# Two lanes of images: stating the first three blocks of a lane's next image ahead of the other lane's bilinear block

## The chip, the cores and the metric

The kernel runs on one core of a Trainium2 chip. The metric is device time in microseconds (us) of one execution. Three runs of the kernel before gave 13435.75, 13443.8 and 13488.92 us; their median, 13443.8 us, is the time before.

## What is computed

Sixteen images of 56 x 56 pixels and 128 channels, all float32, pass one after the other through four residual layers. Each layer normalizes its input by groups of four channels, applies a block and adds the result back:

```python
x = x + _L0(_gn(x), ...)   # attention in shifted 7x7 windows, 4 heads
x = x + _L1(_gn(x), ...)   # triangle multiplication: gated projections, one 56x56 product per channel, layer norms
x = x + _L2(_gn(x), ...)   # Fourier attention over channels and two spectral operators with GELU
x = x + _L3(_gn(x), ...)   # bilinear: per-pixel 16x8 and 16x16 products of convolved keys and values
return x
```

The images do not touch each other anywhere, so the order in which they are worked on is free. Within an image every layer needs the whole result of the layer before.

## The kernel before, in words

An image stays in on-chip memory as a tile `xt` (128 channels x 3136 pixels) from its load to its store. There are two **lanes**; image b belongs to lane b mod 2 (`lane[0] = b % 2`, line 466). Each lane has buffers of its own: one large scratch tile, the arena (lines 321 and 335), five 512-column work tiles (`w2`), twelve scratch buffers in device memory (`dram`), two small PSUM buffers (`psb`) and one double-size PSUM buffer (`psd`). The pool of image tiles has two buffers that the lanes share (line 320). Since a lane has one arena and every block takes it anew, the blocks of one lane follow each other. Only work of the other lane can stand beside them, so there are at most two images in flight.

The four blocks, with the names used below:

- **Window attention** (`_window_attention`, lines 480 to 612): eight rows of windows. TensorE makes queries, keys, values and scores (line 563 is the score product), VectorE does the softmax, ScalarE copies.
- **Triangle** (`_triangle`, lines 615 to 726): many small TensorE products (line 678 makes the gated projections) and VectorE gates (lines 689 and 690).
- **Fourier** (`_fourier`, lines 729 to 1273): after attention over channels (line 1093), an inner loop of 64 steps. Each step fetches two pieces of a coefficient table by GpSimd DMAs (line 1200), multiplies them on VectorE (line 1202) and sums on TensorE (line 371, the helper `together`). It ends with two spectral operators and adds its parts to `xt` at lines 1253 and 1271.
- **Bilinear** (`_bilinear`, lines 1276 to 1472): seven chunks of 448 pixels. `project` (line 1317) makes queries, keys and values and writes copies to device memory by DMAs on ScalarE's queue. `spread` (line 1372) reads shifted planes back on SyncE's queue. `contract` (line 1399) reads a query or kernel tile back four times on SyncE's queue (line 1408), multiplies on VectorE (line 1411, 84 instructions for each image) and sums on TensorE. `last` (line 1426) stores the chunk (line 1445), so this block also writes the output.

What sets the order: the program only states instructions. When it is built, a scheduler walks them with an estimate of each duration and places each on its engine's list when its operands and buffers would be there. Among instructions that could go next on an engine, the one stated earlier goes first. The lists are fixed from then on, and each engine takes its own list in order. The statement order of the images is therefore a priority. In the kernel before, all four blocks of image b are stated ahead of everything of image b+1 (lines 465 to 472):

```python
    for b in range(NB):
        lane[0] = b % 2
        xt = load_image(b)
        done = False
        for s in stages:
            done = run[s](b, xt)
```

Of the kernel before, what the change touches and what calls it, by code (L numbers as in the profile page):

```python
# [307 lines left out]
def tile_blocks(ctx: ExitStack, tc: tile.TileContext, ins, out, at, stages=(0, 1, 2, 3)):  # L308
    nc = tc.nc
    x_in = ins["x"]  # L310
    NB = x_in.shape[0]
# [16 lines left out]
    lane = [0]  # L328
    count = [0]

    def uid(s):
        count[0] += 1
        return f"{s}{count[0]}"
# [4 lines left out]
    def w2():  # L338
        return w2p[lane[0]].tile([P, 512], F32, tag="w2", name=uid("w2_"))
# [4 lines left out]
    def psb():  # L344
        return ps1[lane[0]].tile([P, 512], F32, tag="ps1", name=uid("psb"))
# [37 lines left out]
    def W(name):  # L383
        rows, o, n = at["wgt"][name]
        return wgt[:rows, o : o + n]
# [47 lines left out]
    def load_image(b):  # L433

        xt = xpool.tile([P, NTOK], F32, tag="xt", name=uid("xt"))
        for q in range(NCH):
            t = w2()
            tv = t[:TT, :].rearrange("p (a c) -> p a c", a=4)
            nc.sync.dma_start(
                out=tv,  # L440
                in_=xf[b, q * CH : (q + 1) * CH, :].rearrange("(a p) c -> p a c", p=TT),
            )
            p = psb()
            for a in range(4):
                nc.tensor.transpose(p[:, a * TT : (a + 1) * TT], tv[:, a, :], ident[:TT, :TT])
            act(xt[:, q * CH : (q + 1) * CH], p[:, :CH], AF.Identity, bias=W("bout0"))
        return xt

    def store_image(b, xt):
        for q in range(NCH):  # L450
            p = psb()
            for a in range(4):
                o = q * CH + a * TT
                nc.tensor.transpose(p[:TT, a * P : (a + 1) * P], xt[:, o : o + TT], ident)
            t = w2()
            nc.scalar.copy(t[:TT, :], p[:TT, :])
            nc.sync.dma_start(
                out=of[b, q * CH : (q + 1) * CH, :].rearrange("(a p) c -> p a c", p=TT),
                in_=t[:TT, :].rearrange("p (a c) -> p a c", a=4),
            )  # L460
# [1 line left out]
    env = dict(locals())  # L462
    blocks = [_window_attention, _triangle, _fourier, _bilinear]
    run = {s: blocks[s](env) for s in stages}
    for b in range(NB):
        lane[0] = b % 2
        xt = load_image(b)
        done = False
        for s in stages:
            done = run[s](b, xt)  # L470
        if not done:
            store_image(b, xt)


class _Env:
# [1008 lines left out]
def _build(inputs, bacc, stages=(0, 1, 2, 3)):  # L1484
    x = np.ascontiguousarray(inputs["x"])
    w, early, late = _weights({k: v for k, v in inputs.items() if k != "x"})
    arrays, at = {"x": x}, {}
    for name, parts in (("cst", _constants()), ("wgt", w), ("early", early), ("late", late)):
        arrays[name], at[name] = _pack(parts)
    nc = bacc.Bacc("TRN2", target_bir_lowering=False, num_devices=1)  # L1490
    ins = {k: nc.dram_tensor(k, v.shape, F32, kind="ExternalInput").ap() for k, v in arrays.items()}
    out = nc.dram_tensor("out", x.shape, F32, kind="ExternalOutput").ap()
    with tile.TileContext(nc, schedule_with_timeline_sim=True) as tc:
        tile_blocks(tc, ins, out, at, stages)
    return nc, arrays, out, at
```

## Time and profile before

| What | Value |
|---|---|
| median of three runs | 13443.8 us |
| the profiled execution | 13405.75 us, span 13403.8 us |
| TensorE matmul busy | 10585.8 us, 79% of the span |
| VectorE busy | 9623.6 us, 72% |
| ScalarE busy | 3845.7 us, 29% |
| GpSimd busy | 1426.4 us, 11% |
| moved by DMA | 2105.94 MB, 157 GB/s on the mean |
| granted TensorE clock, mean | 0.847 of full speed |

The page divides the span into 40 slices and gives each engine's busy share in tenths. The pattern repeats about every five slices, once for each pair of images, eight pairs in all. The trace also answers for any stretch of time: busy time of each engine, the granted clock, and the share of the DMA engines in use. Where the stretch is limited to one line of the program, it counts that line's instructions, and so shows which block is at work and how far it gets. Two marks place the images in time: the DMAs of line 439 (seven for each image, its load) and those of line 1445 (seven for each image, its store).

### The profile page before, as it was taken

The page shows a single profiled execution, that of the slowest core. Times are in us where ns is not written, and L with a number is a line of the kernel's source. Part 1 is how long each engine was busy: PE and PEld are TensorE (multiplying, and loading weights), DVE is VectorE, ACT ScalarE, POOL GpSimd, SP SyncE. Part 2 cuts the span into 40 slices and gives each one's busy share as a digit, 9 for nine tenths or more (in the row PEclk, how much of TensorE's full clock was granted, in tenths as well). Part 3 has the DMA queues.
Part 4 walks back from the last instruction along what each step waited for, and adds up shares of the span by engine and source line. Part 5 has one row for each costly group of instructions (what it writes and reads, how often), then busy time and mean ns, then how long its engine had stood idle before and what let it go on. Part 6 is the DMA issues. An engine that isn't in the chain of part 4 may idle for free. (4 is left out here: it accounts for less than half of the span.)

```text
span 13403.8 us, 202422 instructions
## 1 busy us (share of the span) xinstructions
PE 10585.8 (79%) x82624; PEld 5860.7 (44%) x82624; DVE 9623.6 (72%) x13985; ACT 3845.7 (29%) x6638; POOL 1426.4 (11%) x2746
## 2 busy tenths in 40 slices
PE   7887687876878778887778877888778887788776
PEld 4454254542544335443355433554335443354432
DVE  7776868667677686676766667767777677866776
ACT  3223141321423224232242222422224232242221
POOL 0120002200022000220002200022000220002200
PEclk9988898878988889888888778888888888888887
DMA  1256904468044680447804468044780447704577
GB/s 35 73 164 230 315 1 118 118 244 300 1 124 124 237 294 9 118 138 240 276 10 118 131 228 291 13 118 130 245 279 10 118 136 252 270 7 118 131 249 267
DMA packets 1091758, 2105.94 MB, mean 157 GB/s; under 512 B 98320, under 2 KB 974096, under 8 KB 1089680
## 3 DMA queue, kind: packets, MB, share of 16 engines
q1 hardware_dynamic: 560000, 823.95, 18.7%
q0 software_dynamic: 165120, 629.61, 17.1%
q10 hardware_dynamic: 365712, 639.44, 13.2%
q8 instruction: 654, 10.72, 0.3%
q14 instruction: 272, 2.23, 0.1%
HBM read 1412.73 MB, written 667.03 MB: 155 GB/s over the span
## 5 line engine op out<-in xcount | busy, mean ns | idle before, releaser
L1411 DVE TENSOR_TENSOR arena<-arena 128x1792 f32<-128x1792 f32 x1344 | 2661.8, 2018 | 724.6 <-DMA arena<-dy 329.5
L1202 DVE TENSOR_TENSOR arena<-arena 112x1344 f32<-112x1344 f32 x1024 | 1569.5, 1552 | 356.8 <-DMA arena<-table 341.1
L371 PE MATMUL psb<-arena,cst 128*32 128x448 f32 x9792 | 1578.0, 672 | 0.0
L368 PE MATMUL psb<-arena,cst 128*32 128x448 f32 x1408 | 818.8, 670 | 799.9 <-DVE arena L1411 750.3
L1200 POOL DMA_DIRECT2D arena<-table x2048 | 1063.7, 521 | 2799.3 <-PE psb L1116 724.8
L371 PE MATMUL psb<-arena 112*64 112x224 f32 (+2 forms) x4864 | 1245.2, 525 | 0.0
L368 PE MATMUL psb<-arena 112*64 112x448 f32 (+1 forms) x1280 | 691.4, 625 | 369.2 <-DVE arena L1093 187.5
L371 PE MATMUL psd<-arena 112*64 112x224 f32 (+1 forms) x3072 | 749.4, 465 | 0.0
L368 PE MATMUL psd<-arena 112*64 112x448 f32 x1024 | 554.5, 627 | 211.4 <-DVE arena L1202 190.9
L1093 DVE TENSOR_TENSOR arena<-w,coef 128x1792 f32<-128x1792 f32 x256 | 507.6, 2020 | 210.7 <-PE psb L371 187.4
L371 PEld LDWEIGHTS psb<-arena 112*64 112x64 f32 (+1 forms) x4864 | 435.6, 153 | 509.7 <-issue 507.3
L368 PEld LDWEIGHTS psb<-arena,cst 128*32 128x32 f32 x1408 | 118.4, 119 | 1154.3 <-DVE arena L1411 869.2
L678 PE MATMUL psd<-wgt,arena 128*64 128x128 f32 x7168 | 514.4, 293 | 112.4 <-DVE arena L690 96.5
L371 PEld LDWEIGHTS psb<-arena,cst 128*32 128x32 f32 x9792 | 367.6, 125 | 471.4 <-issue 451.0
L1396 ACT COPY arena<-psd 128x896 f32<-128x896 f32 x336 | 303.4, 905 | 930.8 <-DVE arena L1411 549.4
L678 PEld LDWEIGHTS psd<-wgt,arena 128*64 128x64 f32 x7168 | 450.0, 145 | 217.1 <-issue 129.2
L907 PE MATMUL psb<-cst,arena 128*128 128x64 f32 (+1 forms) x2688 | 454.9, 341 | 92.4 <-ACT arena L917 63.2
L371 PE MATMUL psd<-arena,wgt 128*32 128x448 f32 x2688 | 500.6, 604 | 34.4 <-DMA arena<-padded 34.0
L907 PEld LDWEIGHTS psb<-cst,arena 128*128 128x128 f32 x2688 | 437.2, 254 | 148.8 <-ACT arena L917 74.0
L1313 ACT COPY w<-psb 128x448 f32<-128x448 f32 x336 | 178.6, 532 | 1089.1 <-PE psb L371 761.8
L368 PE MATMUL psd<-arena,wgt 128*32 128x448 f32 x896 | 438.6, 607 | 42.4 <-DMA arena<-padded 37.4
L371 PEld LDWEIGHTS psd<-arena 112*64 112x64 f32 x3072 | 287.0, 151 | 284.4 <-issue 283.0
(299 smaller groups left out, 19594.2 us busy)
## 6 DMA issues: line engine op xcount, KB each, us to landing
arena<-table POOLq DMA_DIRECT2D x2048, 294.0 KB, 8.7
dy<-w ACTq DMA_DIRECT2D x336, 1792.0 KB
arena<-dy SPq DMA_DIRECT2D x1344, 448.0 KB
arena<-padded SPq DMA_DIRECT2D x896, 162.8 KB
w<-x SPq DMA_DIRECT2D x112, 224.0 KB
out<-w SPq DMA_DIRECT2D x112, 224.0 KB
padded<-w ACTq DMA_DIRECT2D x336, 62.0 KB
arena<-arena POOLq DMA_DIRECT2D x16, 784.0 KB, 9.8
```

Source lines behind the costliest of these rows:

```text
L368: done = mm(**first)
L371: mm(**kw)
L678: mm(p[half : half + 64, i // 4, i % 4 * P : (i % 4 + 1) * P], lhsT=xh[:, c0 : c0 + 64], rhs=W(w).rearrange("p (k c) -> p k c", c=64)[:, : ...
L907: mm(p[:, 2 * i * nl : 2 * (i + 1) * nl], lhsT=src[:, t * P : (t + 1) * P], rhs=fc, start=True, stop=True)
L1093: tt(t4, bc(ys[c][:, l0 : l0 + 4, :], 1, 8), bc(coef[:, c, h0 : h0 + 8, l0 : l0 + 4], 3, T), ALU.mult,)
L1200: nc.gpsimd.dma_start(out=t[hh * T : (hh + 1) * T, :], in_=bc(tflat[q, two, hh], 0, T))
L1202: tt(t4, bc(x3[:, :, s], 1, 2), t4, ALU.mult)
L1313: nc.scalar.copy(t[:, :CH], p[:, :CH])
L1396: nc.scalar.copy(z, p[:, :, :CH])
L1411: tt(t4, bc(rep, 2, 2), bc(z, 1, 2), ALU.mult)
```

## The change

The loop over images is split in two functions. `first(b)` loads image b and states its first three blocks; `second(b)` states its bilinear block. The loop states `second(b - 2)` and then `first(b)`:

```diff
-    for b in range(NB):
+    early = [s for s in stages if s < 3]
+    late = [s for s in stages if s >= 3]
+    images = {}
+
+    def first(b):
         lane[0] = b % 2
-        xt = load_image(b)
-        done = False
-        for s in stages:
+        images[b] = load_image(b)
+        for s in early:
+            run[s](b, images[b])
+
+    def second(b):
+        lane[0] = b % 2
+        xt, done = images.pop(b), False
+        for s in late:
             done = run[s](b, xt)
         if not done:
             store_image(b, xt)
+
+    for b in range(NB + 2):
+        if b >= 2:
+            second(b - 2)
+        if b < NB:
+            first(b)
```

With F for load and first three blocks and B for the bilinear block, the order of statement was F0 B0 F1 B1 F2 B2 F3 B3 and so on. It becomes F0 F1 B0 F2 B1 F3 B2 F4 and so on, ending with F15 B14 B15. Within a lane nothing changes its place: lane 0 is F0 B0 F2 B2 in both. No instruction is added or removed, and no buffer changes. What changes is which lane goes first where one lane has a B and the other an F to do: before, the lower image number; now, the F.

## The prediction

> **What bounds the kernel now.** I read the page's first two parts, then stretches of time by engine and by line, then the waits, then SyncE's timeline.
>
> ```profile
> span 13403.8 us, 202422 instructions
> ...
> PE 10585.8 (79%) x82624; PEld 5860.7 (44%) x82624; DVE 9623.6 (72%) x13985; ACT 3845.7 (29%) x6638; POOL 1426.4 (11%) x2746
> ...
> DVE  7776868667677686676766667767777677866776
> ...
> DMA  1256904468044680447804468044780447704577
> ```
>
> No engine is full over the span. The DMA row runs 0, 4, 4, 6 to 7, 8 in every five slices, again and again: the two lanes go through the same blocks at nearly the same time. That comes to one pair of images in about 1655 us: the first loads of lane 0 (line 439) stand at 18, 1587, 3243, 4824, 6431, 8165, 9822 and 11478 us, and lane 0 stores last at 13142. Lane 1 loads 7, 72, 94, 191, 263, 213, 222 and 217 us after lane 0. So lane 0's lead grows to about 220 us and stays there.
>
> Now six stretches, named by what the lanes do: both in bilinear (first pair), lane 0 in window attention beside lane 1's bilinear end, lane 0 in bilinear beside lane 1's Fourier end, both in bilinear (last pair), and image 15 alone in bilinear.
>
> ```profile
> core 0: us, PE busy (x) PEld busy (x) DVE busy (x) ACT busy (x) POOL busy (x), PEclk, DMA share, GB/s
> 1144.00:1530.00 386.00, 300.07 (x1853) 130.07 (x1848) 267.36 (x309) 73.57 (x125) 5.57 (x11) 0.85 0.95 336
> 11478.00:11695.00 217.00, 154.53 (x1230) 66.06 (x1222) 175.74 (x187) 49.21 (x86) 14.56 (x16) 0.89 0.81 267
> ...
> 12683.00:12966.00 283.00, 228.51 (x1535) 122.97 (x1535) 191.40 (x349) 91.04 (x158) 9.68 (x16) 0.82 0.61 208
> 12966.00:13142.00 176.00, 130.36 (x772) 53.05 (x772) 130.09 (x157) 30.10 (x53) 5.50 (x6) 0.82 0.89 309
> 13142.00:13400.00 258.00, 162.56 (x976) 58.10 (x976) 163.66 (x121) 31.76 (x49) 1.01 (x2) 0.77 0.75 255
> ```
>
> The same stretches for line 1411, VectorE's product of the bilinear block, 84 for each image:
>
> ```profile
> 1144.00:1530.00 386.00, 222.83 (x115) 0.85 0.95 336
> 11478.00:11695.00 217.00, 125.49 (x64) 0.89 0.81 267
> ...
> 12683.00:12966.00 283.00, 85.74 (x43) 0.82 0.61 208
> 12966.00:13142.00 176.00, 102.92 (x52) 0.82 0.89 309
> 13142.00:13400.00 258.00, 145.10 (x73) 0.77 0.75 255
> ```
>
> This is the heart of it. Two bilinear blocks together make 115 / 386 = 0.298 products per us, or 52 / 176 = 0.295. One alone makes 73 / 258 = 0.283. One beside window attention makes 64 / 217 = 0.295. A second bilinear block adds nothing: with two, the DMA engines are 0.89 to 0.95 busy and every product waits for its data. Beside window attention the same rate is had with the DMA at 0.81, and the other lane gets on too. How far is told by its score product (line 563, 128 records for each image):
>
> ```profile
> 11478.00:11695.00 217.00, 7.03 (x64) 3.89 (x64) 0.89 0.81 267
> ```
>
> 64 of 128: half a window attention, in time in which a second bilinear block would have given nothing. The waits name the same loop, and the timeline of SyncE shows what lane 0's next load stands behind:
>
> ```profile
> PE psb L368 <- DVE arena L1411: 750.3, 335, 11.2
> ...
> DVE arena L1411 <- DMA arena<-dy: 329.5, 157, 10.5
> ```
>
> ```profile
> 1529.77 0.34 SPq L1445 DMA_DIRECT2D out<-w  x1
> ...
> 1586.77 4.23 SPq L439 DMA_DIRECT2D w<-x  x4
> ```
>
> Image 0 is stored at 1529.77, but image 2's load goes out only at 1586.77, after image 1's bilinear transfers on the same list.
>
> **What the skill says.** "Perfetto Trace Analysis", section "Optimization Strategy": where a kernel has several regimes with different busiest engines, "performance may be improved by interleaving those regimes in addition to optimizing within each regime". The trace agrees that there are regimes: DMA 0.95 with both lanes in bilinear, 0.02 from 11708 to 11946 with both in the first two blocks. The same page, "Engine Utilization", gives 358 GB/s as the memory's full rate; the 336 GB/s above are 94% of it. "PSUM — Partial Sum Buffer", section "Engine vs sequencer instructions", says that "ScalarE/VectorE/GpSimdE queues are strict FIFO". That is why statement order matters here: a 2.0 us product (line 1411) placed ahead on VectorE holds up the small instructions of the other lane. "TensorE: Matmul & The Clock Gate", section "What's actually happening", has the clock halved when TensorE has been idle. The trace fits: 0.77 with bilinear alone, 0.92 from 11708 to 11946.
>
> **The change, part by part.** No instruction is added or taken away, so no duration of a row changes. The price is in order only.
>
> 1. F2 against B1 (and every like pair): the load, its seven DMAs on SyncE, the memsets on GpSimd (lines 520, 525, 658) and window attention now go ahead of the other lane's bilinear end. Before, window attention of lane 0 took 195 us in the first pair (VectorE's line 415, one at the head of each block, at 47 and 241) and 285 us in the last (11521 to 11806), where it stood behind bilinear. Lane 0 should get most of these 90 us back in each pair. What is queued behind it: bilinear's read-backs (line 1408) behind seven loads, 0.31 to 0.43 us of SyncE each, some 3 us; and products of line 1411 behind window attention's VectorE work. Image 13's bilinear end then takes perhaps 20 to 60 us longer.
> 2. The load's delay: 1586.77 - 1529.77 = 57 us in the first pair, 43 in the second (3200 to 3243), none later, where loads go out up to 29 us before the last store. It falls on one lane of two: (57 + 43) / 2 = 50 us saved.
> 3. B0 against F1: the Fourier end now goes ahead of bilinear's start. Before, with bilinear ahead, lane 1's Fourier took 702 us in the last pair (line 415 at 12275 and 12977) against 613 and 682 in the first. I count this at nothing; it is hidden as long as bilinear waits for DMAs. If that cover fails, bilinear's start loses up to the same 90 us, half of it for the pair. On GpSimd the table DMAs (line 1200) go ahead of bilinear's memset (line 1360): 0.5 us each, 128 for an image, but spread over the inner loop; counted at nothing as well.
> 4. The lead. In the first pair lane 0 gains about 80 us by the end of Fourier (line 415 at 1051 and 1144) and 136 by the last store (1530 and 1666). Part 1's priority took that back to 72. Now it stays, and part 1 adds to it: I estimate a lead of 130 us at the second pair, 250 at the third, and over 400 from the fourth on, past the length of a bilinear block (456 to 511 us).
> 5. What the lead is worth. As it grows, time with both in bilinear (176 us in the last pair, 231 to 264 in the three before, about 220) goes over into bilinear beside the first blocks. 217 us of that kind gave half a window attention free: half of its 200 us in lockstep, on one lane of two, so 50 us for 217, or 51 for 220. Bounds: nothing, if the added contention eats it, and 111, if the block that goes first runs at about twice that pace. I take 55, a little over the measured mean, since F goes first.
> 6. The end. Image 15's bilinear block stands alone there. It took 258 us after image 14; now the whole block is alone: about 93 us to its first products (line 415 at 1051, lane 1 in bilinear at 1144) and 84 / 0.283 = 297, so 390. Cost 390 - 258 = 132 us.
>
> Sum: the saving of 55 counts half in the second pair and whole in six, 6.5 x 55 = 358. 13406 - 358 - 50 + 132 = 13130 for the profiled execution. The median of the runs stands 38 us (0.28%) above it, so 13130 x 1.0028 = 13167; I say **13165 us**, 2.1% below.
>
> **Rivals.**
>
> *More:* F, going first, runs near the pace it would have alone, the upper bound of step 5. 13406 - 6.5 x 111 - 50 + 132 = 12766, times 1.0028 = 12800. For it: TensorE is 0.71 and VectorE 0.81 busy beside window attention, so there is room. Against: their sum, 1.52, is hardly more than the 1.47 of two bilinear blocks.
>
> *Nothing moves:* the builder's estimate may see little of the DMA's limit, and order decides only where two instructions are ready at once. In the kernel before, strict priority for the lower image gave lane 0 just 80 us in three blocks. The lead then stays near 220 and the time within 0.5%: about 13430.
>
> *Slower:* the lead makes unlike blocks meet that share an engine. With Fourier on lane 0, the triangle of lane 1 took 11949 to 12275, 326 us, against 197 to 207 in the first pair, and pairs with a lead of 220 were no faster than those with 90 (1656 against 1581 and 1656). If a longer lead costs 20 us per pair instead of saving 55, the time is 13406 + 6.5 x 20 - 50 + 132 = 13618, times 1.0028 = 13660. The place is triangle and window attention beside Fourier. It decides from where the saving per pair falls below (132 - 50) / 6.5 = 13 us.
>
> **How the numbers follow.** The forecast gets 0.48, more 0.20, nothing 0.13, slower 0.19. A measurement here can tell about 0.5%, that is 67 us. Faster by over that is the first two, 0.68; same 0.13; slower 0.19. The forecast's own range is 12980 to 13370, from 80 us to 20 us saved per pair. For 8 in 10 the range reaches to the upper bound of step 5 below and most of the way to the slower rival above: 12790 to 13560.
>
> **What would show it.** In the trace after: lane 1's loads trail lane 0's by over 400 us from the fourth pair on; no stretch has both lanes in bilinear in the later pairs, so the DMA row has no 8 or 9 over two lanes of line 1411; line 1411 keeps 0.25 to 0.30 per us beside window attention; window attention of lane 0 is back near 200 us; the load follows the store without the 57 us; image 15 ends alone for about 390 us. Wrong would be a lead that stays near 220, a pair time not below 1640 with a lead over 400 (then step 5 failed), or line 1411 at 0.2 per us beside window attention.

## The result and the profile after

The changed kernel takes 13285.01 us, the median of four runs (13253.57 to 13350.28), against 13466.06 us for the kernel before, the median of its runs by then. The ratio on record is 0.9881, with a 95% interval of 0.9844 to 0.9917: 1.2% faster. (The two medians alone, of four runs each, would give 0.9866.) I had forecast 13165 us and 2.1%. Direction and range held. Most of the working did not, as the trace shows.

The page of the changed kernel (its lines after 465 stand 17 further on; line 1428 is line 1411 of before):

```profile
span 13271.1 us, 202286 instructions
...
PE 10399.7 (78%) x82624; PEld 5727.7 (43%) x82624; DVE 9622.1 (73%) x13985; ACT 3830.6 (29%) x6626; POOL 1451.9 (11%) x2746
...
DVE  7776867767777676776867767677677776767767
...
DMA  1256903559144690446904469044591446804468
...
L1428 DVE TENSOR_TENSOR arena<-arena 128x1792 f32<-128x1792 f32 x1344 | 2657.1, 2018 | 647.6 <-PE psb L371 353.8
```

VectorE's instructions cost what they did: it is busy for 9622.1 us as against 9623.6, and line 1428 takes the same 2018 ns. TensorE's did not: 82624 matmuls keep it busy for 10399.7 us as against 10585.8 before, and the granted TensorE clock is 0.855 on the mean as against 0.847. ScalarE runs 12 instructions fewer, all of them loads of its function tables (146 as against 158), which no statement of the kernel asks for. The DMA row still runs 0, 4, 4, 6, 9 in every five slices, so the two lanes are still close together. The lead that I had expected to grow past 400 us is not there.

How far the lanes are apart is read from the eight block starts of one pair. Line 415 runs once at the head of each block; which image it belongs to follows from the tiles in the built program's lists. These are images 12 and 13 in the timeline of VectorE, in the order window attention (lane 0, lane 1), triangle (0, 1), Fourier (0, 1), bilinear (0, 1). First the kernel before:

```profile
9866.44 0.34 DVE L415 BATCH_NORM_AGGREGATE sm<-sm 128x2 f32<-128x42 f32 x1
10067.31 0.32 DVE L415 BATCH_NORM_AGGREGATE sm<-sm 128x2 f32<-128x42 f32 x1
10158.71 0.31 DVE L415 BATCH_NORM_AGGREGATE sm<-sm 128x2 f32<-128x42 f32 x1
10300.89 0.33 DVE L415 BATCH_NORM_AGGREGATE sm<-sm 128x2 f32<-128x42 f32 x1
10337.95 0.34 DVE L415 BATCH_NORM_AGGREGATE sm<-sm 128x2 f32<-128x42 f32 x1
10609.98 0.34 DVE L415 BATCH_NORM_AGGREGATE sm<-sm 128x2 f32<-128x42 f32 x1
10995.01 0.34 DVE L415 BATCH_NORM_AGGREGATE sm<-sm 128x2 f32<-128x42 f32 x1
11259.43 0.33 DVE L415 BATCH_NORM_AGGREGATE sm<-sm 128x2 f32<-128x42 f32 x1
```

And the changed kernel:

```profile
9879.43 0.34 DVE L415 BATCH_NORM_AGGREGATE sm<-sm 128x2 f32<-128x42 f32 x1
10010.22 0.33 DVE L415 BATCH_NORM_AGGREGATE sm<-sm 128x2 f32<-128x42 f32 x1
10129.71 0.31 DVE L415 BATCH_NORM_AGGREGATE sm<-sm 128x2 f32<-128x42 f32 x1
10231.53 0.34 DVE L415 BATCH_NORM_AGGREGATE sm<-sm 128x2 f32<-128x42 f32 x1
10317.58 0.34 DVE L415 BATCH_NORM_AGGREGATE sm<-sm 128x2 f32<-128x42 f32 x1
10463.75 0.34 DVE L415 BATCH_NORM_AGGREGATE sm<-sm 128x2 f32<-128x42 f32 x1
10936.37 0.34 DVE L415 BATCH_NORM_AGGREGATE sm<-sm 128x2 f32<-128x42 f32 x1
11130.93 0.34 DVE L415 BATCH_NORM_AGGREGATE sm<-sm 128x2 f32<-128x42 f32 x1
```

The lead at window attention is 201 us before and 131 after. With it go the lengths. Lane 1's triangle (fourth line to sixth) falls from 309 to 232 us. Lane 0's window attention (first to third) falls from 292 to 250. Bilinear goes the other way: from its start to the last store, lane 0's takes 543 us as against 500 and lane 1's 495 as against 449. Lane 0's pace does not change in these two executions: from image 4's to image 14's window attention it takes 8251 us before and 8248 after. Lane 1 takes 8361 and 8256: before, it fell back by another 110 us over these five pairs, and now by 8.

So at the end lane 0 stores its last chunk at 13142 us before and at 13137 after, and image 15 stands alone for 258 us before and for 130 after. In these two executions that shorter rest is 128 of the 133 us gained. The stretches of the changed kernel that answer to those of the prediction: bilinear of image 13 beside window attention, bilinear of lane 0 beside Fourier of lane 1, both in bilinear, image 15 alone.

```profile
core 0: us, PE busy (x) PEld busy (x) DVE busy (x) ACT busy (x) POOL busy (x), PEclk, DMA share, GB/s
...
11464.00:11619.00 155.00, 108.20 (x813) 43.17 (x811) 128.26 (x121) 31.44 (x52) 13.78 (x11) 0.80 0.80 263
...
12586.00:12785.00 199.00, 156.89 (x1128) 87.70 (x1126) 136.38 (x301) 74.49 (x131) 9.23 (x15) 0.83 0.51 174
12785.00:13137.00 352.00, 261.77 (x1612) 107.73 (x1612) 248.32 (x265) 60.37 (x102) 4.72 (x9) 0.81 0.91 316
13137.00:13267.00 130.00, 76.93 (x492) 23.52 (x488) 94.64 (x56) 13.11 (x19) 0.00 (x0) 0.76 0.76 255
```

The same for line 1428:

```profile
11464.00:11619.00 155.00, 95.64 (x49) 0.80 0.80 263
12586.00:12785.00 199.00, 37.68 (x19) 0.83 0.51 174
12785.00:13137.00 352.00, 208.78 (x106) 0.81 0.91 316
13137.00:13267.00 130.00, 85.24 (x43) 0.76 0.76 255
```

The rates are near those of before, and two of them somewhat higher: 49 / 155 = 0.32 products per us beside window attention (0.295 before), 106 / 352 = 0.30 with two bilinear blocks (0.30), 43 / 130 = 0.33 alone (0.283). In the last pair the time with both in bilinear grew from 176 to 352 us, where I had expected it to vanish.

### The profile page after: what moved, and what is told of

Read it like the earlier page. It is cut to its first block, busy times and chain, and to the rows that moved or that the text cites. A ratio compares the mean times of both kernels' runs of the same rounds, so it can differ in the third digit from the quotient of the medians.

```text
span 13271.1 us, 202286 instructions
## 1 busy us (share of the span) xinstructions
PE 10399.7 (78%) x82624; PEld 5727.7 (43%) x82624; DVE 9622.1 (73%) x13985; ACT 3830.6 (29%) x6626; POOL 1451.9 (11%) x2746
## 5 line engine op out<-in xcount | busy, mean ns | idle before, releaser
L1428 DVE TENSOR_TENSOR arena<-arena 128x1792 f32<-128x1792 f32 x1344 | 2657.1, 2018 | 647.6 <-PE psb L371 353.8
L371 PE MATMUL psb<-arena,cst 128*32 128x448 f32 x9792 | 1530.0, 658 | 0.0
L368 PE MATMUL psb<-arena,cst 128*32 128x448 f32 x1408 | 806.8, 660 | 708.3 <-DVE arena L1428 658.5
L371 PE MATMUL psb<-arena 112*64 112x224 f32 (+2 forms) x4864 | 1212.9, 509 | 0.0
L371 PE MATMUL psd<-arena 112*64 112x224 f32 (+1 forms) x3072 | 786.2, 484 | 0.0
L368 PE MATMUL psd<-arena 112*64 112x448 f32 x1024 | 582.9, 656 | 238.7 <-DVE arena L1219 213.7
L606 PE MATMUL psb<-cst,arena 128*49 128x128 f32 x2048 | 346.1, 326 | 129.2 <-DVE arena L601 87.6
```

Source lines behind the costliest of these rows:

```text
L368: done = mm(**first)
L371: mm(**kw)
L606: nc.tensor.transpose(p[:WIN, i * P : (i + 1) * P], s3[:, 4 * g + i, :], C("ident"))
L1428: tt(t4, bc(rep, 2, 2), bc(z, 1, 2), ALU.mult)
```

## The experiments

All ratios are to the kernel before on the same chip. The lead is taken at window attention from the third pair on. The pair time is a fifth of the time from image 4's to image 14's window attention, meaned with the same for images 5 and 15, from one profiled execution. Two pair times that differ by some 12 us can't be told apart: e10_after_hold has the order of the changed kernel and its leads, and shows 1662 in its profiled execution, the slowest of its six runs, as against 1650. The edits below are against the changed kernel; only `e1_pairs` shows the loop that is replaced, and of the longer edits only the telling lines stand here.

| Kernel | Lead, us | Pair time, us | Ratio, 95% interval |
|---|---|---|---|
| before | 86 to 253, then 200 | 1661 | 1 |
| changed | 125 to 133 | 1650 | 0.9881 (0.9844 to 0.9917) |
| e1_pairs | 122 to 271 | 1684 | 0.9993 (0.9974 to 1.0012) |
| e2_half | 87 to 327 | 1675 | 1.0055 (1.0036 to 1.0074) |
| e3_lastpair | 89 to 252, then 195 | 1669 | 0.9983 (0.9961 to 1.0006) |
| e4_blocks | 62 to 89 | 1684 | 1.0030 (1.0012 to 1.0049) |
| e5_long | 1077 to 1188 | 1668 | 1.0382 (1.0338 to 1.0426) |
| e6_notlast | 124 to 133 | 1650 | 0.9913 (0.9882 to 0.9943) |
| e7_before_late | 315 to 347 | 1683 | 1.0218 (1.0189 to 1.0247) |
| e8_after_late | 321 to 337 | 1679 | 1.0144 (1.0113 to 1.0175) |
| e9_before_hold | 88, then 140 to 144 | 1654 | 0.9955 (0.9938 to 0.9971) |
| e10_after_hold | 123 to 132 | 1662 | 0.9900 (0.9868 to 0.9931) |
| e11_mix | 75 to 89 | 1690 | 1.0092 (1.0059 to 1.0125) |
| e12_pairs_hold | 119 to 142 | 1671 | 0.9952 (0.9933 to 0.9970) |

### Each half of the change alone

The change holds two rules: F1 goes ahead of B0, and F2 ahead of B1. Each was stated without the other. e1_pairs:

```diff
-    for b in range(NB + 2):
-        if b >= 2:
-            second(b - 2)
-        if b < NB:
-            first(b)
+    for b in range(0, NB, 2):
+        first(b)
+        first(b + 1)
+        second(b)
+        second(b + 1)
```

> Order F0 F1 B0 B1 F2 F3 B2 B3: of the change only 'F1 ahead of B0' is kept, 'F2 ahead of B1' is gone. Theory 'short lead' (the change gains because F1 ahead of B0 holds lane 0 back in its bilinear block, so lane 1 trails by less at the end, while the pace of lane 0 stays as it was): lane 0's bilinear stays near 555 us, the lead at the end is 130 us or less, time 13200 to 13320, ratio to before 0.985 to 0.992. Theory 'overlap' (the change gains because F2 goes ahead of B1 and window attention runs beside bilinear; this is the one of the prediction): nothing of the gain is left, ratio 0.995 to 1.005.

Measured: 13427.7 us, 0.9993. Through the second pair each block keeps within about 10 us of its length in the changed kernel. Then lane 0's window attention, now behind B1, takes 265 to 335 us, the lead runs up to 271, and the gain is gone. Lane 0's bilinear does not stay near 555 us, though F1 still goes ahead of B0: from its start to the lane's next window attention it takes 499 to 546 us for images 4 to 10, as against 574 to 588 in the changed kernel. e2_half:

```diff
+    first(0)
+    second(0)
+    for b in range(1, NB - 1, 2):
+        first(b)
+        first(b + 1)
+        second(b)
+        second(b + 1)
+    first(NB - 1)
+    second(NB - 1)
```

> Order F0 B0 F1 F2 B1 B2 F3 F4 B3 B4: only 'F2 ahead of B1' is kept, 'F1 ahead of B0' is gone. Short lead: lane 0 is favoured everywhere, the lead grows past the 260 us of before, lane 0's bilinear is back near 500 us, time 13440 or more, ratio 1.000 to 1.015. Overlap: this half carries the gain, ratio 0.985 to 0.992.

Measured: 13506.94 us, 1.0055. The lead grows to 327 us, as "short lead" had said, and the rule that I had counted on for the whole gain makes the kernel slower when it stands alone. Both theories lose one of the two runs: "overlap" falls here, and "short lead" did not foresee that e1_pairs would lose its lead.

### A shorter and a much longer lead

e4_blocks states the blocks of a pair by turns:

```diff
+        for s in early:
+            for k in pair:
+                lane[0] = k % 2
+                run[s](k, images[k])
+        for k in pair:
+            second(k)
```

> The blocks of a pair of images stated by turns: window attention of both, triangle of both, Fourier of both, bilinear of both. Short lead: the lanes are kept within some 60 us of each other, the last image ends less than 80 us after the one before it, time 13150 to 13280, ratio 0.978 to 0.988. Overlap: the two bilinear blocks stand together for all of their length, the worst arrangement, ratio over 1.003.

Measured: 13471.09 us, 1.0030. The lanes were kept together, and the last image ended 90 us after the other, but the time did not fall: "shorter is better" is wrong. e5_long starts lane 1 late:

```diff
         xt = xpool.tile([P, NTOK], F32, tag="xt", name=uid("xt"))
+        if other is not None:
+            nc.scalar.copy(xt[:, NTOK - 1 : NTOK], other[:, 0:1])
...
-        images[b] = load_image(b)
+        images[b] = load_image(b, images[0] if b == 1 else None)
```

> The statement order of the changed kernel; one added copy of one column makes image 1's last load step wait for the end of image 0's Fourier block, so that lane 1 starts some 600 to 800 us late and every bilinear block stands beside the other lane's first three blocks. The end is 13271 plus what the late start costs, so the pair time in the middle is what counts, not the total. Overlap: the pair time in the middle falls from 1645 to under 1600 us, line 1428 (the bilinear product) keeps 0.25 to 0.3 per us beside the other lane's window attention, total 13300 to 13700. Short lead: the pair time stays at 1630 to 1660 us, total 13700 to 14000.

Measured: 13959.51 us, 1.0382. The DMA row of its page no longer has the zeros of lockstep:

```profile
DMA  1425318454283544745265551836428354474437
```

The lanes are over 1000 us apart and no bilinear block meets another, just what the prediction had wanted. The pair time is 1668 us as against 1661. In its middle stretch the engines do no more than before (here also the first three blocks of image 0, alone):

```profile
core 0: us, PE busy (x) PEld busy (x) DVE busy (x) ACT busy (x) POOL busy (x), PEclk, DMA share, GB/s
47.00:901.00 854.00, 535.22 (x3844) 320.54 (x3844) 421.53 (x655) 186.18 (x323) 84.15 (x168) 0.74 0.20 51
3066.00:11452.00 8386.00, 6602.43 (x51710) 3644.32 (x51708) 6007.80 (x8766) 2507.39 (x4239) 911.18 (x1716) 0.85 0.50 157
```

TensorE 6602 / 8386 = 0.79 and VectorE 0.72. The same stretch of before has 0.80 and 0.72:

```profile
3270.00:11521.00 8251.00, 6573.54 (x51216) 3652.83 (x51216) 5916.01 (x8647) 2403.83 (x4139) 893.46 (x1709) 0.84 0.49 155
```

Lane 0's bilinear block falls from a mean of 501 us to 420, but its window attention rises from 280 to 358 and its triangle from 185 to 217. What bilinear wins by standing beside other blocks, those blocks lose. "Overlap" falls. (The total also holds the late start, so it is the pair time that counts here.)

### Is it the end, or is it every pair?

e3_lastpair takes only the last pair in the changed order; e6_notlast has all pairs but the last in it.

```diff
+    for b in range(NB - 2):
+        first(b)
+        second(b)
+    first(NB - 2)
+    first(NB - 1)
+    second(NB - 2)
+    second(NB - 1)
```

> Images 0 to 13 as in the kernel before; only the last pair is stated F14 F15 B14 B15. Theory 'end' (half of the change's gain or more lies in the last pair, where F15 ahead of B14 lets image 15 end sooner): the last image ends 110 to 190 us after the one before it instead of 258, ratio to before 0.992 to 0.997. Theory 'steady pace' (the gain is made pair by pair, by both rules together): ratio 0.998 to 1.002.

```diff
+    for b in range(NB - 1):
+        if b >= 2:
+            second(b - 2)
+        first(b)
+    second(NB - 3)
+    second(NB - 2)
+    first(NB - 1)
+    second(NB - 1)
```

> The changed kernel, with B14 stated ahead of F15 again, as before; all other pairs in the changed order. End: lane 0 ends some 50 us sooner and image 15 stands alone for over 200 us, ratio 0.992 to 0.997. Steady pace: ratio 0.986 to 0.990, as the change itself.

Measured: 0.9983 with an interval that holds 1, and 0.9913. By these ratios the swap at the end would be worth 0.2 to 0.3%, which is not clear of the intervals. The traces agree on the size: from image 14's window attention to the end it is 1883 us before and 1843 in e3_lastpair, 1804 in e6_notlast and 1770 in the changed kernel, so 40 and 34 us for the swap (in e6_notlast image 15 stands alone for 187 us, in the changed kernel for 130). The larger part was gathered before the last pair. The first is in the range of "steady pace", the second between the two theories.

### Is the lead held by the order?

In e7_before_late and e8_after_late, image 1's last load step waits for the end of image 0's window attention; e7 has the order of before, e8 the changed one.

```diff
         for s in early:
+            lane[0] = b % 2
             run[s](b, images[b])
+            if (b, s) == (0, 0):
+                lane[0] = 1
+                images[1] = load_image(1, images[0])
```

> The kernel before, with lane 1 started late: image 1's last load step waits for the end of image 0's window attention (one added copy of one column). It tells whether the lead is held by the order or only handed on from the start. Held by the order: the lead of before, 200 to 260 us at the window block, is there from the first pairs on and stays; time 13440 to 13560, ratio 1.000 to 1.009. Handed on: the lead is longer by the delay, some 150 us, all through, and the ratio is 1.008 or more.

> The changed kernel, with lane 1 started late in the same way. Held by the order: the lead comes back to 120 to 150 us within a few pairs and the time stays below that of before, ratio 0.986 to 0.995. Handed on, or the gain owed to one lucky list of the builder: the lead stays over 200 us, ratio 0.998 or more.

Measured: 1.0218 and 1.0144. Neither order brings its lead back. Image 1's window attention starts 192 us after image 0's, the lead is 332 and 326 us one pair later, and some 330 us stay to the end. Both lose: a lead of this size is handed on from pair to pair under either order. (Not every lead is: before, it grew from 0 in the first pair to 253 us in the fifth, and then stood near 200.) The starts of window attention (lanes 0 and 1) and of lane 0's triangle in e8_after_late, images 12 and 13:

```profile
9949.60 0.34 DVE L415 BATCH_NORM_AGGREGATE sm<-sm 128x2 f32<-128x42 f32 x1
10272.55 0.33 DVE L415 BATCH_NORM_AGGREGATE sm<-sm 128x2 f32<-128x42 f32 x1
10305.79 0.34 DVE L415 BATCH_NORM_AGGREGATE sm<-sm 128x2 f32<-128x42 f32 x1
```

Lane 0's window attention takes 356 us although it is stated ahead of bilinear; in e7_before_late, stated behind it, the mean is 361. So at this lead its length hardly depends on which is stated first. At about one and the same lead the two orders differ by 0.7%: 13622.91 against 13713.34 us. But this is no steady gain for each pair. Of the 123 us between the two profiled executions, 77 have been gained by image 4's window attention, 26 in the five pairs after it, and 20 after image 14's.

### The lead alone

e9_before_hold keeps the order of before, and makes lane 0's next image wait for lane 1's second bilinear chunk:

```diff
+        if b % 2 == 0 and b >= 4:
+            nc.scalar.copy(xt[:, NTOK - 1 : NTOK], mark)
...
             nc.scalar.copy(y[:, :CH], acc[:, :CH])
+            if b % 2 and q == 1:
+                nc.scalar.copy(e.mark, y[:, 0:1])
```

> The kernel before in its own order, with lane 0 held: from image 4 on, the last load step of lane 0's image waits until lane 1's bilinear block has made its second chunk (two added copies of one column), which keeps the lead near the 130 us of the changed kernel. Nothing else is taken from the change. Theory 'lead' (what the change gains it gains through a lead near 140 us in place of 220 to 260): lane 1's triangle falls from 306 to 240 us or less, ratio to before 0.987 to 0.995. Theory 'rule' (it gains because the first three blocks go ahead of bilinear, whatever the lead): ratio 0.999 to 1.008, since lane 0 only loses time by the wait.

Measured: 13369.27 us, 0.9955 (0.9938 to 0.9971), outside the range of "lead" by 0.0005 and well outside that of "rule". A lane that is only made to wait makes the kernel faster, and the lead is then 140 to 144 us. The starts of window attention (lanes 0 and 1), of lane 1's triangle and of lane 1's Fourier, images 12 and 13 (line 416 here is line 415 of before):

```profile
9859.66 0.34 DVE L416 BATCH_NORM_AGGREGATE sm<-sm 128x2 f32<-128x42 f32 x1
10002.95 0.33 DVE L416 BATCH_NORM_AGGREGATE sm<-sm 128x2 f32<-128x42 f32 x1
10239.12 0.34 DVE L416 BATCH_NORM_AGGREGATE sm<-sm 128x2 f32<-128x42 f32 x1
10516.44 0.34 DVE L416 BATCH_NORM_AGGREGATE sm<-sm 128x2 f32<-128x42 f32 x1
```

Lane 1's triangle falls to 231 us for image 7 and to 277 to 281 after that, a smaller fall than expected. The gain is a bit over a third of the change's. That it comes through the lead is the reading of theory "lead"; the added copies also give the builder another list to make, and that was not tested apart.

e10_after_hold has the changed order and waits for the fifth chunk (`q == 4`).

> The changed kernel, with lane 0 held until lane 1's fifth chunk, so that the lead at the window block falls to about 60 us. Lead: a shorter lead is no better, since then both Fourier inner loops and both bilinear blocks fall together as with the blocks stated by turns; pair time 1660 to 1690, ratio 0.996 to 1.006. Rule: the time stays with the change, ratio 0.986 to 0.993.

Measured: 0.9900. The wait did not bind: the lead stayed at 123 to 132 us, so nothing is learned on a shorter lead. The run stands as a second measurement of the changed order. The changed kernel, this one and e6_notlast are three builds with this order in all pairs or in all but the last, at 0.9881, 0.9900 and 0.9913, so the gain is not owed to one lucky list of the builder.

e11_mix was a try at a better order:

```diff
+    for b in range(0, NB, 2):
+        some(b, (0, 1))
+        if b:
+            second(b - 1)
+        some(b + 1, (0, 1))
+        some(b, (2,))
+        some(b + 1, (2,))
+        second(b)
+    second(NB - 1)
```

> A try at a better order: window attention and triangle of each lane go ahead of the other lane's Fourier and bilinear blocks, and Fourier of lane 1 ahead of lane 0's bilinear. Lead: it depends on where the lead settles; with lane 1's triangle no longer behind lane 0's Fourier, triangle of lane 1 near 200 us and a lead of 100 to 140, ratio 0.980 to 0.992. Rule: more of what the change does, ratio 0.978 to 0.988.

Measured: 1.0092. The lead settles at 75 to 89 us, as in e4_blocks, and both are slower than before. No kernel tried beats the changed one.

e12_pairs_hold joins the order of e1_pairs and the hold of e9_before_hold.

> The order F0 F1 B0 B1 of e1_pairs (only 'F1 ahead of B0' kept) with the hold of e9_before_hold on lane 0, which keeps the lead near 140 us. Theory 'lead and one rule' (the change gains by its lead, and by F1 ahead of B0, which shortens lane 1's Fourier from some 706 to 675 us): ratio 0.986 to 0.993, as the changed kernel. Theory 'both rules needed' (F2 ahead of B1 brings something that the hold doesn't): ratio 0.994 to 1.000, no better than e9_before_hold.

Measured: 0.9952, in the range of "both rules needed". At window attention the lead was 119 to 142 us, about that of the changed kernel, although lane 0's load led by 137 to 141 us in four pairs and by 194 to 198 in two. With this lead and F1 ahead of B0 the kernel is no faster than with the lead alone. That points to F2 ahead of B1 for the rest, but the wait itself may cost something here, so it isn't settled.

## Why the prediction was right in its sign and wrong in its steps

That direction and range held was luck: the forecast took its gain from a longer lead, and the gain that came goes with a shorter one.

**Step 1** (lane 0's window attention gets most of 90 us back) failed. It fell from a mean of 280 to 255 us. On the mean of images 6 to 14 alone it is 291 us before, 268 in e9_before_hold (order of before, lead 140 to 144 us) and 256 in the changed kernel. So most of the fall comes with the shorter lead, and going first brings at most 12 us; at a lead of 330 us (e8 against e7) it brings 5. The cost to the other lane's bilinear end, 20 to 60 us, came out at 46 (449 to 495 us for image 13). From its start to the lane's next window attention that block takes 510 us on the mean, as against 464 in e9_before_hold, so here it goes with the order and not with the lead. The two late kernels show no such cost.

**Step 2** (50 us from the delayed load) was a misreading. I took the store at 1529.77 us for image 0's last. By the tiles in the list it belongs to image 1; image 0's last is the one at 1598.86, after the load:

```profile
1586.77 4.23 SPq L439 DMA_DIRECT2D w<-x  x4
...
1598.86 0.92 SPq L1445 DMA_DIRECT2D out<-w  x1
```

The trace agrees: image 2 is first written into the tile that image 0 leaves at 1597.04 (ScalarE, line 446). There was no delay to save. Stores of two lanes on one queue can't be told apart by line.

**Step 3** (F1 ahead of B0, counted at nothing) failed. Lane 0's bilinear takes 555 us as against 501, close to the loss that I had named for the case that the cover fails. Without this rule lane 0 runs ahead: e2_half has a lead of up to 327 us. Alone it doesn't hold lane 0 back either: e1_pairs keeps it, lane 0's bilinear gets short again, and the lead reaches 271 us.

**Step 4** (the lead grows past 400 us) failed: 125 to 133 us, shorter than before.

**Step 5** (a longer lead saves 55 us per pair) failed, as the term that carried the sum. That "every product waits for its data" was said too strongly: the line shown has 157 waits for that DMA, and there are 1344 products. That a second bilinear block adds nothing to the rate of line 1411 held (0.30 as against 0.33 alone), and so did the rate beside window attention. But window attention and triangle pay for it. From a lead of 130 to one of 330 us, within the changed order, the bilinear blocks of the two lanes get 87 and 77 us shorter, while window attention and triangle together get 95 and 104 us longer, and lane 0's Fourier 25. The slower rival had the right sign, and its price of 20 us per pair is near what e7 shows in the order of before: 1683 as against 1661. Its place was right in part. At a lead of 200 us lane 1's triangle is the one that pays; from there to 330 it is window attention, of lane 0 beside bilinear (280 to 361 us) and of lane 1 (235 to 281). The rival was attached to a lead that the change does not make.

**Step 6** (132 us lost at the end) failed with the lead: 128 us were gained there.

In place of these steps, the runs show the following. With the order of before, a lead of some 140 us gives 0.9955, one near 200 gives 1, and one of 330 gives 1.0218, late start included (e9_before_hold, before, e7_before_late). With the changed order, 130 us gives 0.9881 and 330 gives 1.0144. So the change gains in part through the shorter lead: a hold that brings it to 140 us is worth 0.45%. The rest goes with the two rules together; neither gains alone (e1_pairs, e2_half). It can't be read off e8 against e7 as 0.7% to be added to 0.45%, since most of those 0.7% come before image 4. Between e9_before_hold and the changed kernel, at nearly equal leads, 63 of the 79 us in the profiled executions come after image 14's window attention, 18 before image 4's and none between them. So in these executions the rules show mostly at the start and in the last pair. How they do it stays open.

Why a lead near 130 to 140 us is good is read from the traces and not tested further. From 200 us on lane 1's triangle stands beside lane 0's Fourier (300 us as against 237). At 85 us both Fourier inner loops and both bilinear blocks fall together (lane 0's Fourier takes 671 us in e4_blocks as against 625), but the two kernels with that lead, e4_blocks and e11_mix, also have orders of their own.

One rival stands untested, the granted TensorE clock. Within one and the same kernel the time follows it: of 28 runs of before in one series, the two with a mean clock of 0.842 took 13482.92 and 13490.66 us, and the one with 0.852 took 13351.07. The four runs of the changed kernel have 0.850 to 0.857, and the one with 0.850 took 13350.28 us. The five runs of before with 0.850 took 13372.6 to 13429.69, on the mean 13400. That comparison, of one run with five and between two series, leaves 0.4% of the 1.2% at equal clock. The mean over the runs is 0.846 to 0.847 for before, 0.854 for the changed kernel, 0.851 for e9_before_hold, and 0.8345 and 0.837 for e7 and e8. The order in which blocks meet may itself decide what clock is granted, or both may follow from something else. No run here holds one and changes the other, so through what the shorter lead and the two rules save time is not shown.

## What to carry to other kernels

Where two chains share the engines, first measure how far apart they run and what each block costs at that distance. A rate that one block keeps beside another says nothing of what the other pays, so sum both lanes' block lengths before calling an overlap free. A fixed order can hand a distance on from one round to the next, as it did with 330 us here. So a wait on the chain that runs ahead can make the whole faster, and a rule that holds it back should be priced, not counted at nothing. And where the granted clock differs between two kernels, compare runs at the same clock before a gain is put down to the order alone.

## What was not expected of the hardware

In these runs the work done per time hardly depends on how the lanes stand to each other. With leads from 75 to 1190 us the pair time stays within 1650 to 1690 us, 2.4%, though DMA use ranges from a clear rhythm of 0 to 9 tenths to an even one. The three first blocks of image 0 take 854 us with nothing beside them, and 1005 beside image 1's; one lane alone has TensorE at 0.63 and VectorE at 0.49, two lanes have them at 0.8 and 0.72.
